# Q and three quarters of V as 26 products of sums of blocks in a one-core attention block

## The chip, the cores and the metric

The kernel runs on one core of a Trainium2 chip. The metric is the device time of one execution in microseconds; the time before is the median of three runs.

## The reference, cut to what matters

Two sequences of 512 tokens, width 512, pass through an attention with 32 heads of 128 and then a small gated feed-forward part, all in float32. The change touches only the projections to Q and V:

```python
x = _layernorm(hidden)                 # (2, 512, 512)
q = rms_norm(x @ Wq + bq, gq)          # (2, 512, 4096), normed over all 4096
k = rms_norm(x @ Wk + bk, gk)
v = x @ Wv + bv
attn = softmax(q_h @ k_h.T * scale)    # for each of 32 heads
out = (attn @ v_h) @ Wo + bo
x = hidden + _layernorm(out)           # then the feed-forward part
```

## The kernel before

The work runs in stages. First the tokens of each sequence are normed and transposed into four tiles of 128 features by 512 tokens (`norm_transposed`, L150). Then `project` (L194) makes Q, and after it K, in eight chunks `g` of four heads. A chunk is the product of both sequences' tokens with 512 weight columns. It is done by seven products of sums of 2x2 blocks instead of eight: `weight_sums` (L183) makes four sums of weight blocks on GpSimd, `token_sums` (L172) makes four sums of token blocks on VectorE once, in the opening of the q stage, and VectorE adds the products up as it reads them from PSUM (L278 to L301). Each of the seven is two heads `j` by two matmuls `c`, so that a chunk is 28 matmuls of 128x128 by 128x512. Every finished head goes to HBM (`keptq`, `keptk`, L237), ScalarE squares it (L235) and GpSimd adds the squares to `accq` or `acck` (L236), from which the norm over 4096 comes. These squares go through `tmp`, four tiles.

Other work is laid beside the q stage: `value_sums` (L322) loads blocks of Wv, makes four sums of them on GpSimd and stores them in `keptw`; `output_sums` (L348) does the like for Wo on VectorE (`keptwo`). Beside the k stage, Q is scaled (`scalings`, L368, two of the steps at each call of `between`) and stored again in `keptqs`.

V is made by `values` (L433), as a list of steps. For each of four parts `p` of 1024 columns, 14 entries of seven kinds of product with two token tiles each give 28 steps, each of two matmuls (L458) with a later exit by VectorE or ScalarE (L466 to L486). Of these 112 steps 28 run ahead of the head loop, 28 in the first eight iterations, and 56 in the 36 iterations after.

The head loop (L696) has 64 iterations, one for a head of one sequence. TensorE makes the scores of the next head (L515), a small matmul for the softmax's sum (L548), V steps and products with Wo (`through_wo`, L615, L621, again seven for eight), and then the weighted values (L571). ScalarE copies the scores (L516) and takes the exponential (L562); VectorE finds the maximum (L525, L526), subtracts it (L559) and sums (L534, L542); GpSimd reduces the maximum over partitions (L528). The products with Wo leave PSUM by ScalarE (L627) and are added in SBUF by DMAs that GpSimd issues (L628).

The order on TensorE, VectorE, ScalarE and GpSimd is the order in which the program issues (`IN_ORDER`, L25). The order on SP, the queue of most DMAs, is the scheduler's. PSUM has eight banks of 128x512 float32, taken by turns.

## Time and profile before

| What | us |
|---|---|
| median of three runs | 1321.91 (1321.35 to 1324.21) |
| the profiled execution | 1322.88 |
| its span, first to last instruction | 1321.1 |
| TensorE busy | 1294.2 (98%) |
| VectorE busy | 973.5 (74%) |
| ScalarE busy | 533.4 (40%) |
| GpSimd busy | 481.7 (36%) |
| first product of the q stage starts | 12.52 |
| first product of the k stage starts | 208.20 |
| first V product starts | 402.19 |

In a line of the profile, PE, DVE, ACT, POOL and SP are TensorE, VectorE, ScalarE, GpSimd and SyncE; PEld is TensorE's weight load. A float32 matmul shows as two records. In a timeline or in the chain, the first number is the start in us from the span's start and the second is the length in us; `x8` counts instructions drawn together; the bracket at the end gives the idle time of that engine just before, and what ended it. L numbers are lines of the kernel before.

### The profile page before, as it was taken

To read this page: it belongs to the slowest core of one execution; us is meant where nothing else is said; L and a number is where in the kernel's file an instruction comes from. 1 tells how busy PE (TensorE), PEld (TensorE's weight loads), DVE (VectorE), ACT (ScalarE), POOL (GpSimd) and SP (SyncE) were. 2 spreads that over 40 slices of the span, in tenths; PEclk is the share of its full clock that TensorE was granted. 3 is DMA by queue.
4 is the path that set the end of the run, shared out by engine and by line. 5 is a ranking of instruction groups with operands and counts; after the bars stand their busy time and mean duration, and the time that the engine had idled before them with its cause. 6 is when DMAs were issued, how large, how long until landed. Compare 5 with 4: busy or idle time off the path is not lost.

```text
span 1321.1 us, 11827 instructions
## 1 busy us (share of the span) xinstructions
PE 1294.2 (98%) x3532; PEld 651.5 (49%) x3532; DVE 973.5 (74%) x1235; ACT 533.4 (40%) x732; POOL 481.7 (36%) x368
## 2 busy tenths in 40 slices
PE   7999999999999999999999999999999999999996
PEld 3444444444444444455555555555555555544453
DVE  7565654888565478888777786886877887899666
ACT  5222222322221234354444545455444566544253
POOL 3799897556762011111123231322322322211002
PEclk9999999999999999999999999999999999999999
DMA  8799978599997765533456566566557565520101
GB/s 288 240 326 310 338 268 273 199 342 309 321 344 265 248 199 181 180 120 98 153 152 183 141 182 160 140 183 168 161 151 197 132 156 139 146 64 24 36 5 64
DMA packets 146127, 250.45 MB, mean 190 GB/s; under 512 B 11792, under 2 KB 39568, under 8 KB 146064
## 3 DMA queue, kind: packets, MB, share of 16 engines
q1 hardware_dynamic: 135408, 230.31, 52.3%
q0 software_dynamic: 10080, 18.35, 8.4%
q10 hardware_dynamic: 576, 1.05, 0.2%
q8 instruction: 28, 0.46, 0.2%
q14 instruction: 35, 0.29, 0.1%
HBM read 147.43 MB, written 83.89 MB: 175 GB/s over the span
## 4 chain that ended last, share of the span: by engine, by line
PE 90%; DVE 7%; ACT 2%; DMA 1%; issue 1%; SPq 0%; ACTq 0%; DVEq 0%
PE pss L515 15%; PE o L571 15%; PE v L458 15%; PE p_q L215 15%; PE p_k L215 15%; PE psw L621 10%; PE psy L665 2%; DVE quarters L534 1%; DVE s L559 1%; PE hg L816 1%; ACT s L562 1%; DVE y L655 1%; PE psd L548 1%; PE f L823 1%; DVE m L525 1%
## 5 line engine op out<-in xcount | busy, mean ns | idle before, releaser
L528 POOL PARTITION_ALL_REDUCE top<-m x64 | 119.0, 1860 | 616.8 <-DVE m L526 616.8
L516 ACT ACTIVATE s<-pss,rk 128x512 f32<-128x512 f32 x256 | 175.9, 687 | 320.2 <-PE pss L515 314.7
L571 PE MATMUL o<-s,v 128*128 128x512 f32 x512 | 231.4, 594 | 5.9 <-ACT s L562 2.6
L515 PE MATMUL pss<-qh,kh 128*128 128x512 f32 x512 | 230.2, 592 | 0.0
L515 PEld LDWEIGHTS pss<-qh,kh 128*128 128x128 f32 x512 | 97.3, 190 | 122.5 <-issue 121.5
L571 PEld LDWEIGHTS o<-s,v 128*128 128x128 f32 x512 | 96.2, 190 | 112.0 <-issue 96.9
L534 DVE TRANSPOSE_TENSOR_REDUCE quarters<-s 128x64 f32<-128x2048 f32 x64 | 147.3, 2301 | 0.0
L559 DVE TENSOR_TENSOR s<-s,top 128x2048 f32<-128x2048 f32 x64 | 146.0, 2281 | 0.0
L562 ACT ACTIVATE s<-s 128x2048 f32<-128x2048 f32 x64 | 121.7, 1902 | 13.7 <-DVE s L559 13.6
L458 PE MATMUL v<-w_v,t 128*128 128x512 f32 x256 | 116.8, 600 | 0.0
L550 DVE RECIPROCAL inv<-psd 128x16 f32<-128x16 f32 x64 | 16.4, 256 | 127.5 <-PE psd L548 127.5
L236 POOL TENSOR_TENSOR accq<-accq,sq_q 128x512 f32<-128x512 f32 x62 | 80.9, 1306 | 36.7 <-ACT sq_q L235 35.2
L236 POOL TENSOR_TENSOR acck<-acck,sq_k 128x512 f32<-128x512 f32 x62 | 85.8, 1388 | 21.5 <-ACT sq_k L235 18.3
L235 ACT ACTIVATE sq_q<-q 128x512 f32<-128x512 f32 x62 | 38.9, 630 | 132.8 <-DVE q L288 69.1
L235 ACT ACTIVATE sq_k<-k 128x512 f32<-128x512 f32 x62 | 38.5, 630 | 133.5 <-DVE k L288 66.0
L458 PE MATMUL v<-w_v,nT_a 128*128 128x512 f32 x192 | 88.3, 601 | 0.0
L621 PE MATMUL psw<-wr,oh 128*128 128x256 f32 x384 | 88.3, 380 | 0.0
L215 PE MATMUL p_k<-t,s_k 128*128 128x512 f32 x192 | 85.0, 592 | 0.0
L215 PE MATMUL p_q<-t,s_q 128*128 128x512 f32 x192 | 85.0, 592 | 0.0
L621 PEld LDWEIGHTS psw<-wr,oh 128*128 128x128 f32 x384 | 72.5, 190 | 19.8 <-issue 11.5
L525 DVE TENSOR_TENSOR m<-s 128x1024 f32<-128x1024 f32 x64 | 77.8, 1215 | 4.7 <-ACT s L516 4.7
L458 PEld LDWEIGHTS v<-w_v,t 128*128 128x128 f32 x256 | 46.7, 190 | 49.3 <-issue 49.0
(182 smaller groups left out, 1781.9 us busy)
## 6 DMA issues: line engine op xcount, KB each, us to landing
keptq<-q SPq DMA_DIRECT2D x64, 256.0 KB, 6.4
q<-keptq SPq DMA_DIRECT2D x16, 1024.0 KB, 6.5
w_v<-keptw SPq DMA_DIRECT2D x32, 512.0 KB, 3.9
keptk<-k SPq DMA_DIRECT2D x64, 256.0 KB, 6.6
keptqs<-q SPq DMA_DIRECT2D x64, 256.0 KB, 6.7
qh<-keptqs SPq DMA_DIRECT2D x64, 256.0 KB, 3.0
kh<-keptk SPq DMA_DIRECT2D x64, 256.0 KB, 2.7
keptv<-o_v SPq DMA_DIRECT2D x64, 256.0 KB, 3.8
```

The source lines that it names most:

```text
L215: nc.tensor.matmul(ps, a[:, c, ts(j, P)], x[c], start=(c == 0), stop=(c == 1))
L236: nc.gpsimd.tensor_tensor(accs[b], accs[b], sq, ALU.add)
L458: nc.tensor.matmul(ps, x[c][:, ts(t, P)], w[:, c, :], start=(c == 0), stop=(c == 1))
L515: nc.tensor.matmul(ps, kk[i][:, ts(k, P)], qs[i], start=True, stop=True)
L516: nc.scalar.activation(s[:, k, :], ps, AF.Copy, scale=rks[b][:, k : k + 1])
L525: nc.vector.tensor_tensor(m, s[:, 0:2, :], s[:, 2:4, :], ALU.max)
L528: nc.gpsimd.partition_all_reduce(ms[i], m[:, 0, :], P, ReduceOp.max)
L534: nc.vector.tensor_reduce(quarters.rearrange("p k j -> p (k j)"), ss[i].rearrange("p k (j r) -> p (k j) r", r=32), AX.X, ALU.add, apply_tr ...
L559: nc.vector.tensor_tensor(s, s, top.unsqueeze(1).to_broadcast([P, NT, 512]), ALU.subtract)
L562: nc.scalar.activation(ss[i], ss[i], AF.Exp)
L571: nc.tensor.matmul(po, vs[b, c][:, k, ts(j, P)], ss[i][:, k, :], start=(k == 0), stop=(k == NT - 1))
L621: nc.tensor.matmul(ps[:, t, :], a, right_of[i, g][:, j, :], start=(j == 0), stop=(j == 1))
```

## The change

Q and the parts 0 to 2 of V are no longer made by 28 matmuls for a 2x4 by 4x4 arrangement of blocks, but by 26. One side of a block of work has 2x4 pieces of 128x512 (in V the weights of a part, in Q the transposed tokens of both sequences), the other 4x4 pieces of 128x128 (in V one sequence's tokens, in Q a chunk's weights). `X_ADDS` lists 18 sums of the wide pieces (numbers 8 to 25), `W_ADDS` 28 sums of the narrow ones (16 to 43); "~" also turns the sign. `STEPS` is the order of one block's work, with times in units of a product: 26 products by number, some added onto another's bank, 9 copies out of PSUM on ScalarE, 11 joins on VectorE, all of which read one operand from PSUM, and 8 last sums that give the results. Four of the last sums have both inputs in SBUF.

There are six V blocks (part by sequence), then eight Q blocks, one for a chunk. `values_and_queries` puts every instruction at a time (26 to a block) and issues them sorted by it. Sums of raw Wv pieces go to VectorE and those with a sum in them to GpSimd, and the same for the weight pieces of Q; in the first block the tokens' 28 sums go to VectorE, and the second sequence's are dealt to both by turns. The second sequence is loaded behind Wv on SP, and normed and transposed inside the first block. The pieces of Wq of a chunk are made one block ahead, the wide token sums of Q in the last V block, and the sums of Wv's last part (`value_sums`) and of Wo (`output_sums`, in eight smaller steps) beside the Q blocks. The pieces live in two pools that are given back before the k stage, and six pools of the later stages take their place.

`project` is left with K alone, and makes `token_sums` at its start. `values` is left with part 3: 28 steps, 14 ahead of the head loop and 14 in its first eight iterations. None run after.

The diff, cut to its core:

```diff
+POOLS = (("vpool", 4), ("hpool", 3), ("xpool", 4), ("spool", 3), ("gpool", 2), ("upool", 7))
...
+X_ADDS = (
+    (8, 5, "-", 6), (9, 1, "-", 8), (10, 2, "+", 3), (11, 3, "-", 7), (12, 2, "+", 11), (13, 11, "-", 0),
...
+W_ADDS = (
+    (16, 8, "+", 10), (17, 4, "+", 16), (18, 1, "+", 13), (19, 11, "-", 15), (20, 10, "+", 11), (21, 20, "-", 15),
...
+STEPS = (
+    (0.00, "product", 17, None, 9, 17), (1.00, "product", 22, None, 7, 14), (1.93, "copy", 17),
+    (2.00, "product", 15, None, 10, 18), (2.66, "copy", 22), (3.00, "product", 24, None, 2, 19), (3.41, "copy", 15),
...
+    (24.00, "product", 25, 19, 21, 43), (24.92, "last", 6, "s6", "+", "s8"), (25.00, "product", 4, 10, 25, 0),
+    (26.17, "last", 7, "s7", "-", "s8"), (27.43, "join", 1, "s15", "-", "p1"), (28.68, "last", 1, "s1", "-", "s19"),
+    (29.93, "join", 25, "p25", "-", "s23"), (31.19, "last", 4, "p4", "+", "s25"),
+    (32.44, "last", 0, "s0", "+", "s25"),
...
-            (nc.sync, nc.scalar)[b].dma_start(out=xts[t], in_=x[b, ts(t, P), :])
+            if b == 0:
+                nc.sync.dma_start(out=xts[t], in_=x[b, ts(t, P), :])
         return xts
...
-        if len(xTs) < B:
-            load_next(1)
-            leave = open_chunk(0, "ps")
-            second = norm_transposed(xs[1], "a1", "aux")
-            leave()
-            xTs.append(second())
-            leave = open_chunk(1, "ps")
-            sums.extend(token_sums(xTs))
-            leave()
+        load_next(1)
+        open_chunk(0)()
+        sums.extend(token_sums(xTs))
+        open_chunk(1)()
...
+        def values_and_queries(small_pieces, pieces):
...
+            def add(engine, to, p, op, q):
+                engine.tensor_tensor(to, p, q, ALU.subtract if op == "-" else ALU.add)
+                if op == "~":
+                    nc.scalar.activation(to, to, AF.Copy, scale=-1.0)
...
+                def step(kind, node, *args):
+                    if kind == "product":
+                        on, one, two = args
+                        if on is None:
+                            banks[node], left[node] = free.pop(0), uses[node]
+                        nc.tensor.matmul(banks[root[node]], seconds[two], firsts[one], start=on is None, stop=closing[node, one], skip_group_check=True)
+                    elif kind == "copy":
+                        nc.scalar.copy(tile_of(node), banks[root[node]])
+                        read(node)
+                    else:
+                        p, op, q = args
+                        how = (value(p), ALU.add if op == "+" else ALU.subtract, value(q))
+                        if kind == "last":
+                            finish[0](node, *how)
+                        else:
+                            to = values[node] if p == f"s{node}" else tile_of(node)
+                            nc.vector.tensor_tensor(to, how[0], how[2], how[1])
+                        for v in (p, q):
+                            if v[0] == "p":
+                                read(int(v[1:]))
...
+            def token_piece(b, to, p, op, q, engine):
+                v = tokens[b]
+                v[to] = small_pieces.tile([P, P], F32, tag="s", name=f"x{to}_{b}")
+                add(engine, v[to], v[p], op, v[q])
...
+            def value_piece(p, to, a, op, c, engine):
+                v = wv_pieces[p]
+                v[to] = pieces.tile([P, 512], F32, tag="f", name=f"wv{p}_{to}")
+                add(engine, v[to], v[a], op, v[c])
...
+            def value_out(p, b):
+                def finish(node, first, op, second):
+                    f, t = divmod(node, NT)
+                    pool, tag = ((qpool, "q"), (kpool, "k"))[node % 2]
+                    o = pool.tile([P, 512], F32, tag=tag, name=f"v{p}_{b}_{node}")
+                    nc.vector.tensor_tensor(o, first, second, op)
+                    nc.sync.dma_start(out=keptv[b, 2 * p + f, t], in_=o)
+
+                return finish, lambda node: None
...
+            rows_pieces = {b * NK + k: xTs[b][k] for b in range(B) for k in range(NK)}
+
+            def rows_piece(to, p, op, q, engine):
+                v = rows_pieces
+                v[to] = pieces.tile([P, 512], F32, tag="f", name=f"xr{to}")
+                add(engine, v[to], v[p], op, v[q])
...
+            def query_piece(g, to, p, op, q, engine):
+                v = wq_pieces[g]
+                v[to] = small_pieces.tile([P, P], F32, tag="s", name=f"wq{g}_{to}")
+                add(engine, v[to], v[p], op, v[q])
...
+                def finish(node, first, op, second):
+                    b, j = divmod(node, GH)
+                    h = g * GH + j
+                    o = outs[node] = qpool.tile([P, 512], F32, tag="q", name=f"q{b}_{h}")
+                    nc.vector.scalar_tensor_tensor(o, first, bq[:, h : h + 1], second, ALU.add, op)
+                    nc.sync.dma_start(out=keptq[b, h], in_=o)
+
+                def squared(node):
+                    b, j = divmod(node, GH)
+                    h, o = g * GH + j, outs[node]
+                    if b not in begun:
+                        begun.add(b)
+                        nc.scalar.activation(accq[b], o, AF.Square)
+                    else:
+                        sq = tt(f"sq_q{b}_{h}")
+                        nc.scalar.activation(sq, o, AF.Square)
+                        nc.gpsimd.tensor_tensor(accq[b], accq[b], sq, ALU.add)
...
+            V, G_ = nc.vector, nc.gpsimd
+            nv = B * LATE
+            load_values(0)
+            for t in range(NT):
+                nc.sync.dma_start(out=xs[1][t], in_=x[1, ts(t, P), :])
+            nc.sync.dma_start(out=vec, in_=vecs)
+            (apply0, turn0, leave0), (apply1, turn1, leave1) = (first_norm(b) for b in range(B))
+            for t in range(NT):
+                apply0()
+                turn0()
+            for t in range(NT):
+                leave0(t)
+            for n, a in enumerate(W_ADDS):
+                at(need["w", a[0]] - 6, lambda a=a: token_piece(0, *a, V))
+            for n, a in enumerate(X_ADDS):
+                at(need["x", a[0]] - 6.1, lambda a=a, e=(V, G_)[n > 3 and n % 2]: value_piece(0, *a, e))
+            for t in range(NT):
+                at(2.2 + 2 * t, apply1)
+                at(6.3 + 2 * t, turn1)
+                at(8.4 + 2 * t, lambda t=t: leave1(t))
+            for n, a in enumerate(W_ADDS):
+                at(15.4 + 0.37 * n, lambda a=a, e=(V, G_)[n % 2]: token_piece(1, *a, e))
+            at(2.5, lambda: nc.sync.dma_start(out=row, in_=rows.partition_broadcast(P)))
+            at(20.3, constants)
+            for p in range(1, LATE):
+                at(26 * (2 * p - 2) + 1.5, lambda p=p: load_values(p))
+                for n, a in enumerate(X_ADDS):
+                    at(26 * (2 * p - 1) + 4.3 + 1.05 * n, lambda p=p, a=a, e=(V, G_)[max(a[1], a[3]) >= 8]: value_piece(p, *a, e))
+            for n, a in enumerate(X_ADDS):
+                at(26 * (nv - 1) + 4.3 + 1.05 * n, lambda a=a, e=(V, G_)[max(a[1], a[3]) >= 8]: rows_piece(*a, e))
+            for g in range(NG):
+                n = nv + g
+                at(26 * (n - (2 if g == 0 else 1)) + 0.5, lambda g=g: load_queries(g))
+                for i, a in enumerate(W_ADDS):
+                    raw = max(a[1], a[3]) < 16
+                    at(26 * (n - 1) + 7.2 + 0.68 * i, lambda g=g, a=a, e=(G_, V)[raw]: query_piece(g, *a, e))
+            for c in range(2):
+                at(26 * (nv + 1 + 2 * c) + 3.5, lambda c=c: value_sums(LATE, c))
...
+            for g in range(WG):
+                at(26 * (nv + g) + 0.3, lambda g=g: load_rows(g, rows_of[g % 2]))
+                for i in range(8):
+                    at(26 * (nv + g + 1) + 1.2 + 3 * i, lambda g=g, i=i: output_sums(g, rows_of[g % 2], i))
+            at(26 * (nv + NG - 1) + 0.6, lambda: wk0.append(load_w(wk[:, ts(0, GH * P)], "w_k0")))
+            for p in range(LATE):
+                for b in range(B):
+                    block(2 * p + b, f"v{p}_{b}", wv_pieces[p], tokens[b], value_out(p, b))
+            for g in range(NG):
+                block(nv + g, f"q{g}", rows_pieces, wq_pieces[g], query_out(g))
+            for _, _, work in sorted(events, key=lambda e: e[:2]):
+                work()
...
+        with ExitStack() as scope:
+            pools = [
+                scope.enter_context(tc.tile_pool(name=name, bufs=bufs, reuse_waits="tile"))
+                for name, bufs in (("spieces", 56), ("fpieces", 32))
+            ]
+            values_and_queries(*pools)
+        vpool, hpool, xpool, spool, gpool, upool = (
+            ctx.enter_context(tc.tile_pool(name=name, bufs=bufs, reuse_waits="tile"))
+            for name, bufs in POOLS
+        )
-        for g in project(xTs, sums4, wq, bq, steps[:, 0, :], "q", [(qpool, "q")], keptq, accq, weight_sums(wq0, "q0")):
-            if g == 0:
-                nc.sync.dma_start(out=row, in_=rows.partition_broadcast(P))
-            if g == 2:
-                nc.vector.tensor_scalar(nbthr, bthr, -1.0, None, ALU.mult)
-                nc.vector.tensor_tensor(gqk, vec[:, 3, :], vec[:, 4, :], ALU.mult)
-            if g == NG - 2:
-                k_parts = weight_sums(load_w(wk[:, ts(0, GH * P)], "w_k0"), "k0")
-            value_sums(g // 2, g % 2)
-            if 0 < g <= WG:
-                output_sums(g - 1)
-            if g < WG:
-                load_halves(g)
-        for g in project(xTs, sums4, wk, bk, steps[:, 1, :], "k", [(kpool, "k"), (upool, "u")], keptk, acck, k_parts, between=scale_some):
-            if g == 0:
...
+        k_parts = weight_sums(wk0[0], "k0")
...
-            todo = [(p, tiles, i, x) for p in range(NG // 2) for tiles in ((0, 1), (2, 3)) for i, x in order]
+            todo = [(p, tiles, i, x) for p in (LATE,) for tiles in ((0, 1), (2, 3)) for i, x in order]
...
-        for n in range(28):
+        for n in range(14):
             next(v_steps)()
-            if n in (2, 4):
-                key_scales(n // 2 - 1)
-            if n == 12:
+            if n in (2, 3):
+                key_scales(n - 2)
+            if n == 4:
                 for i in range(3):
                     fetch(i)
-            if n == 18:
+            if n == 7:
                 scores(0)
                 top_of(0)
         for c in range(2):
             for b in range(B):
                 fetch_v(b, c)
         combining, held = [], []
-        left = 28 * (NG // 2 - 1)
+        left = 14
         po = None
...
-            want = 28 * (i + 1) // G if i < G else 28 + 56 * (i + 1 - G) // (5 * G - 4)
-            while left and 84 - left < want:
+            while left and 14 - left < 14 * (i + 1) // G:
```

## The prediction

> **What bounds the kernel now.** I read the page's busy rows first, then the chain of work that ended last in order of time, then timelines of single engines where the change lands.

> ```profile
> PE 1294.2 (98%) x3532; PEld 651.5 (49%) x3532; DVE 973.5 (74%) x1235; ACT 533.4 (40%) x732; POOL 481.7 (36%) x368
> ...
> PE   7999999999999999999999999999999999999996
> ...
> POOL 3799897556762011111123231322322322211002
> ```

> TensorE is never idle after the first slice of 33 us, so only matmuls taken away, or gaps opened in TensorE, move the time. GpSimd is busy in the first ten slices, where the change puts its sums, and nearly idle after.

> ```profile
> 22.80 185.40 PE p_q L215 x432
> 208.20 24.04 PE p_k L215 x56
> ```

> Two lines of the chain in order of time: 432 matmul records in 185.4 us, 0.4286 us each; a float32 128x512 matmul is two records, 0.857 us. The q stage has 448 records (192.0 us) and ends at 208.2, so 16.2 us of it are not products.

> ```profile
> 64.71 0.80 DVE L352 TENSOR_TENSOR wo<-wo 128x512 f32<-128x512 f32 x1
> 65.54 1.64 DVE L353 TENSOR_TENSOR wo<-wo,wo 128x512 f32<-128x512 f32 x1
> 67.21 1.64 DVE L354 TENSOR_TENSOR wo<-wo,wo 128x512 f32<-128x512 f32 x1
> 68.89 1.64 DVE L355 TENSOR_TENSOR wo<-wo 128x512 f32<-128x512 f32 x1
> ...
> 72.62 0.69 DVE L278 TENSOR_TENSOR u_q<-p_q,u_q 128x512 f32<-128x512 f32 x1 [0.90 <-PE p_q L215]
> ...
> 68.27 1.71 POOL L329 TENSOR_TENSOR a_v<-a_v,a_v 128x512 f32<-128x512 f32 x1
> 70.06 1.60 POOL L330 TENSOR_TENSOR s_v<-a_v,a_v 128x512 f32<-128x512 f32 x1
> 71.62 1.27 POOL L331 TENSOR_TENSOR a_v<-a_v,a_v 128x512 f32<-128x512 f32 x1
> ```

> Timelines of VectorE and GpSimd. A VectorE sum with both inputs in SBUF takes 1.64 us instead of 0.69 while GpSimd works, and GpSimd's takes 1.71 instead of 1.27. They take turns, one pair every 1.67 us. L278, which reads PSUM, is not slowed with GpSimd busy.

> ```profile
> 1124.44 3.60 PE L571 MATMUL o<-s,v 128*128 128x512 f32 x8
> ...
> 1134.98 3.60 PE L571 MATMUL o<-s,v 128*128 128x512 f32 x8
> ...
> 1144.59 0.70 PE L571 MATMUL o<-s,v 128*128 128x512 f32 x1 [0.63 <-ACT s L562]
> ```

> TensorE late in the head loop, where no V product is left. A head with two output products (L621) takes 10.54 us (1134.98 less 1124.44), its matmuls' own time; a head with one takes 9.61 and waits for the exponential (L562).

> **The change part by part.** *Products.* A block is 26 matmuls of 128 instead of 28. Eight Q chunks and six V blocks (three parts, two sequences) lose 28 matmuls: **-24.0 us**. The instruction order of the changed kernel shows 364 such matmuls, so this part is certain.

> *Opening.* Before, the first product starts at 12.5 and the 16.2 us include it. After, x0's four loads stand alone at the head of SP's queue (Wv's eight, then x1's four behind them; x1 came by ScalarE's queue), which gains perhaps 1 us; but two wide and two narrow VectorE sums now stand between the transposed tokens and the first product (0.60, 0.69, twice 0.29: 1.9 us). I take 12 to 13. Then VectorE's queue is long. Up to the result that frees the bank for product 8, the fifth product from the block's end, it holds 35 sums of 128x128 (L862 is the row, 0.285 us, four in 0.90, so 0.205 each: 7.2), 11 of 128x512 at 0.60 (6.6), 9 reads of PSUM at 0.60 (5.4), x1's four norms at 1.06 (4.2) and two copies (1.2): 24.6 us. GpSimd makes seven wide pieces meanwhile, and each can hold a VectorE sum up to 1.04 us (1.64 less 0.60): 6 more. From about 10 us that is 40.6; five products and a wait follow, so block 0 ends near 46, against 22.3 us of products. What is queued behind: ScalarE's norms of x1 wait for VectorE, the bank copies stand behind them in order, and TensorE waits for the banks. 23.7 us outside products instead of 16.2: **+7.5**.

> *The shared turns.* GpSimd's 128x128 sum is not in the trace. Bounds: a quarter of the row's 1.27 us is 0.32. [...] I take 0.41 as the pitch. A steady Q block then holds on GpSimd 18 narrow sums (7.4) and 8 square sums (L236, 1.23 apart: 9.8), and on VectorE, with both inputs in SBUF, 4 results (0.55 each), 10 raw weight sums (0.15) and 8 output-weight sums (0.28): 5.9. Together 23.1 us against TensorE's 22.3. In blocks q1 and q3 the value sums add 4 x 1.23 to make 28.0. Over q1 to q6 that is 2 x 5.7 + 4 x 0.8 = 14.6; q0 and q7 have slack, I take **+12**. In the V stage an odd block has 12 wide sums on GpSimd (14.8) and 10 on VectorE (5.5), 20.3: hidden. The last V block also makes the first weight pieces: 22.1 + 7.0 = 29.1, partly wanted late in q0: **+3**.

> [...] Row: a pair costs 1.67 us. [...]

> *VectorE alone* in a Q block: 19 results and joins (8 at 0.66, 11 at 0.60: 11.9) and 18 sums (about 4.6): 16.5 of 22.3, hidden as long as its turns come. ScalarE: 9 copies (0.58) and 8 squares (0.63), 10.3, hidden by the same block.

> *DMA.* 48 stores of V and Wv's loads leave the head loop for the V stage: 3 MB a block, 135 GB/s, hidden. Q: 5 MB a block, 7 in q1 and q3 (314 GB/s; the page's best slice shows 344). SP loads the value pieces in q0 and has them before GpSimd asks. Scaled-Q loads and late V weights that were spread over the q stage now fall into the first k chunk, with the wait for SP that this makes; the first thing wanted behind them, the third k weights, has two chunks (48 us) of cover. Cost nil, 0 to 3 if the cover fails.

> *Start of K.* The token sums (L177 to L180), eight VectorE sums from SBUF, were made in the opening and are now made when K starts, after chunk 0's first results (7.2 us in), while GpSimd makes eight weight sums. At 1.67 us the sixth, which product 6 needs, is done at 17.2; TensorE is there at 14.6: **+2.6** (0 to 6).

> *Head loop.* 1.5 V products a head go from heads 8 to 43. Nine of these heads are left with one output product and take 9.61 us for 8.83 of matmuls: +7.0. Before, six heads (15, 16, 23, 24, 39, 40) lost 3.9 us to late banks, as the 1.49 us wait shows below; VectorE no longer reads V there, so that goes, and the exponential is late next. Heads 0 and 4 keep one V product: +1.5. Net **+4.7**.

> ```profile
> 776.14 1.10 PE L571 MATMUL o<-s,v 128*128 128x512 f32 x2 [1.49 <-ACT w L627]
> ```

> The 14 V steps left ahead of the loop (24 us) still cover the first head's chain (ScalarE 0.69, VectorE 1.9, GpSimd 1.86, VectorE 2.28: under 7 us).

> **Sum:** -24.0 + 7.5 + 12 + 3 + 2.6 + 4.7 = **+5.8**. The profiled execution took 1322.88 us for a span of 1321.1; it lies 1.0 above the median of 1321.91. I put the change on the median: 1327.7, say **1328**.

> **The rivals.**
> 1. *The turns fit (faster).* If the narrow GpSimd sum takes 0.32 or less, a Q block's shared work is 21.5, under 22.3, and the stalls of q0 to q7 shrink to the two value blocks; if VectorE also slips its short sums in between GpSimd's, those go too. Then -24.0 + 4.5 (opening with half the waits) + 4.7, and 0 to 4 for the rest: -15 to -11, about **1309**. The point is 22.3 us of shared work a block. For: POOL has slack in the v stage, and the operations are short. Against: the 1.64 us rows.
> [...]
> 3. *The head loop turns VectorE-bound* without the V products. VectorE needs 8.4 us a head (rows L534, L559, L525, L526, L552, L577, L542, L550) of 9.6. The heads from 43 on show that it does not; no more than +3.
> 4. *It doesn't do what it says:* excluded by the instruction order.

> **How the numbers follow.** The forecast, 1319 to 1338, 0.52; rival 1, 0.27; rival 2 and what lies between, 0.19; rival 3, 0.02. What a measurement here can tell from no change is about 0.2%, 2.6 us: 1319.3 to 1324.5. Of the forecast 0.11 lies inside that, of rival 1 0.01; so faster 0.26, same 0.12, slower 0.62. The range leaves out a tenth on each side: 1306 (below rival 1's middle) to 1350 (short of rival 2).

> **What would show it.** Right: 3476 TensorE records; block 0 ending near 46 us; about 22.5 us a block in V; 25 to 28 us in q1 and q3 with TensorE waiting on a VectorE result; VectorE SBUF sums of 1 to 1.6 us beside GpSimd; two or three us lost 15 us into K; heads at 9.6 and 10.5 from head 8. Wrong: Q blocks all at 22.3 (rival 1), or all above 26 (rival 2), or heads longer than 10.6.

## The result, and the profile after

The changed kernel takes 1354.53 us (median of four, 1350.87 to 1356.81) against 1322.12 of the kernel before beside it: 1.024 times as long, 95% interval 1.0214 to 1.0266. The prediction said 1328, and 1350 at most. The profiled execution took 1354.19 us for a span of 1352.3, 31.2 longer than the 1321.1 of before.

The page after: busy rows, then TensorE's, GpSimd's and the clock's rows of the 40 slices.

```profile
PE 1290.3 (95%) x3476; PEld 641.9 (47%) x3476; DVE 1102.7 (82%) x1479; ACT 584.3 (43%) x840; POOL 553.1 (41%) x513
...
PE   5899999899999999999999999999999999999996
...
POOL 1524578988675655711111223332333223211002
PEclk8899999999999999999999999999999999999999
```

The 3476 records are there, 56 fewer than before. But TensorE is busy for only 3.9 us less (1294.2 less 1290.3) where 24.0 were taken away, and idle for 35.1 us more (1352.3 less 1290.3, against 1321.1 less 1294.2). Part of that is records that got longer, which the clock's row shows; the prediction had no term for it. By stage, from the starts of the blocks on TensorE's timeline (before, K starts at 208.04 and V at 402.02; the 208.20 and 402.19 given above are the ends of the records just before them, so what lay outside products was 16.0 us and not 16.2):

| Stage | before | after | change | predicted |
|---|---|---|---|---|
| products, 14 blocks | | 56 records fewer | -24.0 | -24.0 |
| opening: what lies outside products to the end of block 0 | 16.0 | 31.0 (13.0, then 40.3 less 22.3) | +15.0 | +7.5 |
| V blocks 1 to 5 | 111.4 of products | 117.2 (22.9, 22.3, 22.9, 22.3, 26.8) | +5.8 | +3 |
| Q blocks | 178.3 of products | 192.5 (22.3, 26.2, 23.8, 27.4, 23.4, 23.8, and 45.7 for the last two) | +14.2 | +12 |
| K | 194.0 | 202.7 | +8.7 | +2.6 |
| V steps ahead, head loop, rest | 775.1 | 786.5 | +11.5 | +4.7 |
| sum | | | +31.2 | +5.8 |

*Opening.* TensorE's timeline after; then VectorE's and ScalarE's ahead of the first gap, and two of VectorE's rows further on.

```profile
16.93 1.12 PE L484 MATMUL bank<-wv,x 128*128 128x512 f32 x2 [0.23 <-DVE x L459]
24.45 3.75 PE L484 MATMUL bank<-wv,x 128*128 128x512 f32 x4 [6.39 <-issue]
...
44.94 1.16 PE L484 MATMUL bank<-wv,x 128*128 128x512 f32 x2 [2.62 <-DVE v L564]
46.93 5.49 PE L484 MATMUL bank<-wv,x 128*128 128x512 f32 x6 [0.84 <-DVE c_v L495]
```

```profile
18.12 1.38 DVE L459 TENSOR_TENSOR x<-x,x 128x128 f32<-128x128 f32 x1
19.42 1.75 DVE L459 TENSOR_TENSOR wv<-wv,wv 128x512 f32<-128x512 f32 x1
21.09 0.68 DVE L177 BATCH_NORM_STATS2 st_a<-x 128x6 f32<-128x512 f32 x1
...
29.02 0.69 DVE L526 COPY nT_a<-bank 128x512 f32<-128x512 f32 x1 [1.75 <-PE bank L520]
...
44.12 0.67 DVE L564 TENSOR_TENSOR v<-c_v,bank 128x512 f32<-128x512 f32 x1
```

```profile
18.24 0.31 ACT L461 ACTIVATE x<-x 128x128 f32<-128x128 f32 x1 [6.40 <-DVE x L459]
18.46 0.57 ACT L486 COPY c_v<-bank 128x512 f32<-128x512 f32 x1
22.08 0.29 ACT L180 ACTIVATE rs_a<-mv_a,epst 128x1 f32<-128x1 f32 x1 [3.06 <-DVE mv_a L178]
```

Read VectorE's rows first, then ScalarE's, then TensorE's. A narrow sum takes 1.38 us and a wide one 1.75 beside two wide sums of GpSimd (2.54 us from 18.09 on; just before, VectorE's narrow sum took 0.28 and its wide one 0.68); x1's norm stands behind them on VectorE; ScalarE waits 3.06 for it; the bank copies (L486) stand behind that in ScalarE's order; and TensorE has no free bank for 6.39 us. VectorE in turn waits 1.75 us at 29.02 for x1's transposed tokens, which TensorE made late.

Behind the gaps TensorE is slow: four records take 3.75 us instead of 1.88, and later six take 5.49 instead of 2.74. This is the granted clock (PEclk, last but two of the columns: share of a stretch at full speed) in the same profile:

```profile
20.00:30.00 10.00, 5.55 (x11) 2.80 (x12) 7.63 (x26) 6.77 (x14) 0.62 (x1) 0.66 0.12 46
30.00:40.00 10.00, 10.00 (x33) 4.97 (x32) 9.39 (x21) 1.66 (x3) 5.05 (x5) 1.00 0.09 34
40.00:53.70 13.70, 10.24 (x17) 3.96 (x16) 13.34 (x32) 0.78 (x2) 7.46 (x13) 0.75 0.24 89
53.70:144.00 90.30, 89.69 (x209) 39.35 (x208) 62.52 (x87) 21.10 (x36) 32.25 (x24) 1.00 0.35 122
```

*Q.* TensorE's timeline in q1 and, in its last row, q2; VectorE's and GpSimd's in q1:

```profile
208.63 1.13 PE L484 MATMUL bank<-xr,wq 128*128 128x512 f32 x2 [1.89 <-DVE q L597]
209.59 1.82 PE L484 MATMUL bank<-xr,w_q 128*128 128x512 f32 x2
211.21 1.91 PE L484 MATMUL bank<-xr,wq 128*128 128x512 f32 x2
...
238.43 1.10 PE L484 MATMUL bank<-xr,wq 128*128 128x512 f32 x2 [1.23 <-POOL wq L459]
```

```profile
199.55 1.48 DVE L383 TENSOR_TENSOR wo<-wo,wo 128x256 f32<-128x256 f32 x1
200.96 0.67 DVE L495 TENSOR_TENSOR c_q<-c_q,bank 128x512 f32<-128x512 f32 x1
201.55 3.30 DVE L459 TENSOR_TENSOR wq<-w_q 128x128 f32<-128x128 f32 x3
```

```profile
199.43 1.32 POOL L362 TENSOR_TENSOR a_v<-a_v,a_v 128x512 f32<-128x512 f32 x1
200.71 1.45 POOL L363 TENSOR_TENSOR a_v<-a_v,s_v 128x512 f32<-128x512 f32 x1
202.12 3.86 POOL L609 TENSOR_TENSOR accq<-accq,sq_q 128x512 f32<-128x512 f32 x3
```

Three narrow VectorE sums last 3.30 us beside three wide sums of GpSimd (3.86 us), where one at 208.83, with GpSimd idle, takes 0.28; the join that reads a bank (L495), beside GpSimd's L363, keeps its 0.67. That is what the prediction described, sizes included. In q1 and q3 TensorE waits for a result of VectorE; in q2 and q4 to q6 it waits 0.82 to 1.23 us for a narrow sum of GpSimd itself, as in the row at 238.43.

*K and heads.* Two waits in K, each with slow records behind it, and the first head; TensorE, after.

```profile
380.17 7.97 PE L249 MATMUL p_k<-t,s_k 128*128 128x512 f32 x14 [2.38 <-DVE t L212]
...
539.96 8.80 PE L249 MATMUL p_k<-nT_a,w_k 128*128 128x512 f32 x16 [2.46 <-DVE q L409]
...
602.62 3.70 PE L861 MATMUL o<-s,v 128*128 128x512 f32 x8 [2.28 <-ACT s L852]
```

Fourteen records at full speed are 6.17 us. The first wait was predicted (2.6, fifteen us into K). The second is VectorE waiting for a late load of Q to be scaled, which had been costed at nil; SP's waits from 200 to 570 us show what its issue stood behind, stores of scaled Q that had not landed (us in total, times, longest; the changed kernel, then the kernel before from 200 to 410 us):

```profile
SPq L404 <- DMA keptqs<-q: 43.4, 16, 5.1
```

```profile
SPq L375 <- DMA keptqs<-q: 46.0, 17, 4.7
```

The third wait of TensorE is the exponential of head 0.

### The profile page after: what moved, and what is told of

Its sections match the earlier page's. It is cut to its first block, busy times and chain, and to the rows that moved or that the text cites. A ratio compares the mean times of both kernels' runs of the same rounds, so it can differ in the third digit from the quotient of the medians.

```text
span 1352.3 us, 12232 instructions
## 1 busy us (share of the span) xinstructions
PE 1290.3 (95%) x3476; PEld 641.9 (47%) x3476; DVE 1102.7 (82%) x1479; ACT 584.3 (43%) x840; POOL 553.1 (41%) x513
## 4 chain that ended last, share of the span: by engine, by line
PE 47%; DVE 9%; ACT 4%; issue 1%; ACTq 0%; DVEq 0%
PE o L861 15%; PE pss L805 14%; PE psw L911 8%; PE v L736 3%; ACT s L852 3%; PE psy L955 2%; PE p_k L249 2%; DVE quarters L824 1%; DVE s L849 1%; PE hg L1104 1%; DVE m L815 1%; DVE y L945 1%; PE f L1111 1%; DVE r L842 0%; DVE acc_y L945 0%
## 5 line engine op out<-in xcount | busy, mean ns | idle before, releaser
L861 PE MATMUL o<-s,v 128*128 128x512 f32 x512 | 233.1, 598 | 11.9 <-ACT s L852 11.7
L484 PE MATMUL bank<-wv,x 128*128 128x512 f32 x264 | 126.1, 621 | 14.8 <-issue 6.4
L484 PE MATMUL bank<-xr,wq 128*128 128x512 f32 x256 | 124.5, 601 | 9.1 <-DVE q L597 5.0
L852 ACT ACTIVATE s<-s 128x2048 f32<-128x2048 f32 x64 | 121.8, 1904 | 24.3 <-DVE s L849 24.2
L270 POOL TENSOR_TENSOR acck<-acck,sq_k 128x512 f32<-128x512 f32 x62 | 85.3, 1380 | 29.8 <-ACT sq_k L269 26.9
L609 POOL TENSOR_TENSOR accq<-accq,sq_q 128x512 f32<-128x512 f32 x62 | 85.7, 1398 | 16.6 <-ACT sq_q L608 16.0
L484 PEld LDWEIGHTS bank<-wv,x 128*128 128x128 f32 x264 | 51.2, 198 | 82.0 <-issue 66.2
L484 PEld LDWEIGHTS bank<-xr,wq 128*128 128x128 f32 x256 | 48.7, 192 | 73.4 <-issue 53.7
L486 ACT COPY c_v<-bank 128x512 f32<-128x512 f32 x54 | 31.4, 585 | 89.5 <-PE bank L484 89.5
```

The costliest lines, as they stand in the source:

```text
L484: nc.tensor.matmul(banks[root[node]], seconds[two], firsts[one], start=on is None, stop=closing[node, one], skip_group_check=True)
L609: nc.gpsimd.tensor_tensor(accq[b], accq[b], sq, ALU.add)
L852: nc.scalar.activation(ss[i], ss[i], AF.Exp)
L861: nc.tensor.matmul(po, vs[b, c][:, k, ts(j, P)], ss[i][:, k, :], start=(k == 0), stop=(k == NT - 1))
```

## The experiments

Runs 1 to 9 are single executions. They are read by their stages; their totals come from three chips and are not set against each other. A stage varies by itself: where the code of the opening is that of the changed kernel, block 0 took 37.7 to 40.8 us, and the last V block 25.1 to 26.9. Theory A: each stage pays for its own stalls, of the named queue, and the half clock comes on top.

**1. Q without GpSimd's sums of squares.**

```diff
                         nc.scalar.activation(sq, o, AF.Square)
-                        nc.gpsimd.tensor_tensor(accq[b], accq[b], sq, ALU.add)
```

> The changed kernel without GpSimd's sums of the squares of Q (the line accq + sq; the squares themselves are still made, their sum is left out). Theory A (VectorE's SBUF sums and GpSimd's take turns, and in q1 to q5 both together want more than TensorE's 22.3 us): 62 sums of 1.23 to 1.5 us leave GpSimd, 8 or so a block, so the shared work falls from 23 to some 13 us a block, in q1 and q3 from 28 to 18; every Q block at 22.3, q1 and q3 too (26.2 and 27.4 now), the Q stage about 13 us shorter (191.7 to 178 or 179) and its granted clock 1.00 throughout; the whole about 1341. Theory B (the blocks wait for PSUM banks, ScalarE's copies or the transfers of the value sums, GpSimd only stands beside): q1 and q3 stay above 25, the whole within 3 us of 1354. [...]

Measured: Q blocks of 22.3, 23.3, 22.3, 23.7, 22.3, 22.3 and together 44.6 for the last two; the stage 181.0 instead of 192.5, granted clock 1.00 (0.98 in the changed kernel). Groups of VectorE in q1 to q7, the changed kernel first (after the bar: busy us, mean ns of one; then idle time before):

```profile
L459 DVE TENSOR_TENSOR wq<-w_q 128x128 f32<-128x128 f32 x60 | 26.4, 456 | 13.8 <-DMA w_q<-in_wq 13.8
L383 DVE TENSOR_TENSOR wo<-wo,wo 128x256 f32<-128x256 f32 x24 | 19.4, 807 | 0.0
L597 DVE SCALAR_TENSOR_TENSOR q<-c_q,vec,bank 128x512 f32<-128x512 f32 x21 | 15.6, 743 | 1.5 <-PE bank L484 0.3
```

```profile
L597 DVE SCALAR_TENSOR_TENSOR q<-c_q,vec,bank 128x512 f32<-128x512 f32 x21 | 15.6, 745 | 1.9 <-PE bank L484 1.3
L459 DVE TENSOR_TENSOR wq<-w_q 128x128 f32<-128x128 f32 x60 | 17.5, 308 | 16.4 <-DMA w_q<-in_wq 16.4
...
L383 DVE TENSOR_TENSOR wo<-wo,wo 128x256 f32<-128x256 f32 x24 | 10.6, 441 | 0.0
```

With GpSimd's wide sums gone, the same VectorE sums fall from 456 to 308 ns and from 807 to 441; results that read a bank stay at 743 and 745. Of the stage's 14.2 us, 11.5 hang on GpSimd's sums of squares, 3.4 of them as half clock that did not come. So it is theory A, and banks and copies (B) are out as the main cause. But the run takes away two things at once, the turns and the time that these sums hold GpSimd's own queue, in which the narrow sums that TensorE waits for stand; it does not part them. Of the rest, q1 has a wait of 0.71 us for GpSimd and q3 two for ScalarE's copies (0.24 and 0.70).

**2. Filling the wait in K with matmuls.**

```diff
         open_chunk(1)()
+        warm = pt("warm")
+        for n, cols in enumerate((512, 512, 256)):
+            nc.tensor.matmul(warm[:, 0:cols], xTs[0][n][:, 0:P], xTs[1][n][:, 0:cols], start=True, stop=True)
```

> The changed kernel with three extra matmuls (512, 512 and 256 columns, 2.14 us of records, results read by nobody) on TensorE just where it waits 2.38 us for the token sum t2 at the start of K. Theory A (the wait costs twice: its own length, and then 14 records at half clock because TensorE stood idle): the extra work costs nothing, the wait falls to 0.3 us or less, the next 14 records take 6.1 us and not 7.97, and the K stage ends 1.8 us sooner (202.9 to 201.1). Theory B (the slow records have another cause, a late bank or the clock being cut for the load's sake): the records behind still take 8 us, K is as long as it was or 2 us longer.

Measured: the wait 0.23, the fourteen records 6.28 instead of 7.97, as theory A has it; the K stage 201.6, with a wait of 3.33 for the late load further on. But the run doesn't show what it was made for: runs 6, 8 and 9 have the whole wait of 2.36 to 2.38 and also 6.28. The slow records come in some executions and not in others, with the same wait. That is taken up under the hardware below.

**3. The opening without the token sums of sequence 0.**

```diff
                 v = tokens[b]
+                if b == 0:
+                    v[to] = v[p]
+                    return
```

> The changed kernel without the 28 token sums of sequence 0 (VectorE, 128x128, and the sign change on ScalarE; raw pieces take their place in the products, so block 0's and later sequence-0 V results are of other data). Theory A (block 0 of 40.7 us is VectorE's queue in order: sums, x1's norms behind them, ScalarE behind those, the banks behind ScalarE): 7.2 us leave VectorE's queue and with them one stall's half clock, block 0 takes 30 to 34. Theory B (the eight Wv transfers, or GpSimd's seven wide sums one behind the other, set it): 39 to 41. Theory C (TensorE's own order, its banks, sets it): 40 to 41. The other blocks unchanged to 0.5 us.

Measured: block 0 takes 29.2 instead of 40.3, a little more gain than theory A had; the other V blocks 22.9, 22.3, 22.9, 22.3, 25.1. 7.2 us less in VectorE's queue gave 11.1, and block 0 has no half clock. Transfers (B) and TensorE's own order (C) fall.

**4. The V steps and the sums of head pairs dealt otherwise.**

```diff
-        for n in range(14):
+        for n in range(10):
             next(v_steps)()
...
-            if n == 4:
+            if n == 3:
...
-            if n == 7:
+            if n == 6:
                 scores(0)
...
+        v_at = {0: 3, 11: 1, **{i: 2 for i in range(1, G)}}
...
-            while left and 14 - left < 14 * (i + 1) // G:
+            for _ in range(v_at.get(i, 0)):
...
-            if n4 == 0 and 0 < c <= 2 * WG:
-                head_sums(c - 1)
+            if n4 == 1 and 0 < c <= 2 * WG:
+                half_sums = head_sums(c - 1)
+            if n4 in (1, 3) and 0 < c <= 2 * WG:
+                next(half_sums)
```

> The changed kernel with its 28 steps of the last part of V dealt otherwise: 10 ahead of the head loop and not 14, 3 in head 0 as the kernel before had there, 2 in each of heads 1 to 7, 1 in head 11; scores of head 0 one step sooner; and the four sums of head pairs cut in two halves, in the second and the fourth of the four heads and not all in the first. The work is the same. Theory A (the head loop lost 11.5 us because V's products that covered the exponential are gone: 2.28 in head 0, 3.1 in heads 4, 8 and 12 behind the sums of head pairs, 0.75 in each head with a single output product): the 2.28 us wait goes, heads 4, 8 and 12 lose under 0.3 each, one head of 9.61 less; V and heads 5 to 7 us shorter than 786.4, the whole about 1348. Theory B (the loop is VectorE's and each head is as long as VectorE's work in it): 784 to 787, the loss only moves to other heads. Theory C (fewer steps ahead uncover the first head's chain of scores, maximum, exponential): a new wait of 3 to 6 us before head 0, and nothing gained.

Measured: V and heads 779.0 instead of 786.5, 7.5 less. Head 0 waits no more; heads 4, 8 and 12 take 10.53, 10.65 and 10.54 instead of 12.04, 11.70 and 11.11 (head 7 now 11.28). Eleven heads with one output product stay at 9.60. Theory A; the run does not part its three edits. In the same run the late load in K cost a wait of 5.83.

**5. K: token sums first, the load of Q issued later.**

```diff
-        open_chunk(0)()
+        leave = open_chunk(0)
         sums.extend(token_sums(xTs))
+        leave()
...
-                if j == GH - 1 and n + 3 < NG * B:
-                    four_of(n + 3)
+                if j == 1 and 0 < n < NG * B - 2:
+                    four_of(n + 2)
```

> The changed kernel with two edits of order in the K stage, no work changed: the eight token sums stand on VectorE ahead of the results of the first K chunk and not behind them, so they can run while TensorE makes that chunk; and the load of the next four Q heads to be scaled is issued two scalings later, when the stores that it must wait for have landed, so that SP does not stand behind them. Theory A (the two waits of TensorE in K, 2.38 us for t2 and 2.46 to 5.8 us behind a late scaled-Q load, with some 1.8 us of half clock after each, are the 8.9 us that K lost): both waits under 0.3 us, the K stage 194 to 196 us and not 202.9, granted clock 1.00 in it. Theory B (GpSimd, busy with eight weight sums at that point, holds VectorE's token sums up wherever they stand): the wait at t2 moves to the results of the first chunk and to the banks, K 200 or more. Theory C (the transfers themselves are late, not their issue): the second wait stays, K about 199.

Measured: K 197.0 instead of 202.7, clock 1.00. The waits did not go to 0.3 but to 1.20 and 1.21, the first moved to the chunk's results as B has it (L284 in the line, TensorE), and no half clock came behind them:

```profile
377.87 3.67 PE L249 MATMUL p_k<-t,s_k 128*128 128x512 f32 x8 [1.20 <-DVE k L284]
```

The late load is judged over all runs. With the old issue, TensorE waited in late K in seven executions out of nine: 2.46 in the changed kernel, 5.09, 3.33, 1.55 and 5.83 in runs 1 to 4, 3.73 in run 7, 5.07 (there for K's weights) in run 9; only 0.29 in run 6 and nothing in run 8, where K took 197.2 and 196.9. With the later issue (runs 5, 10, 11) it was 1.21, 0.22 and nothing. So the issue that stands behind a store not yet landed is the likely cause, as far as three executions against nine can show, and how late it is varies. In the kernel before, SP waited as long for the same stores (46.0 us) and TensorE did not wait; what took that cover away was not tried.

**6. The value sums in q0 and q7.**

```diff
-                at(26 * (nv + 1 + 2 * c) + 3.5, lambda c=c: value_sums(LATE, c))
+                at(26 * (nv + (0, 7)[c]) + 3.5, lambda c=c: value_sums(LATE, c))
```

> The changed kernel with the two groups of four value sums (GpSimd, 128x512, with their loads and stores) in q0 and q7 and not in q1 and q3. Theory A (shared turns of VectorE and GpSimd): q1 and q3 fall from 26.2 and 27.4 to the 23.8 of q2 and q4, so 6 us less there; q0 and q7, which have no output-weight sums, keep under 24, so the Q stage is 4 to 6 us shorter. Theory B (the loads and stores of the value sums on SP and the DMA queues set q1 and q3): the same gain there, but q0 and q7 grow by as much, because the transfers go with the sums. Theory C (a stall there has nothing to do with them): q1 and q3 stay at 26 and 27.

Measured: Q blocks 22.3, 25.3, 23.5, 23.5, 23.4, 23.5, 23.4, 22.3, the stage 187.3, 5.2 less, of which 3.4 is half clock that did not come. q3 falls by 3.9 as A has it, q0 and q7 don't grow, so it isn't the transfers. q1 keeps 25.3: it waits 1.22 us for a result and 1.29 for a weight sum of GpSimd. That the sums pushed into q0 delay these is likely, but not shown.

**7. The squares added by transfers.**

```diff
-                        nc.gpsimd.tensor_tensor(accq[b], accq[b], sq, ALU.add)
+                        nc.gpsimd.dma_start(out=accq[b], in_=sq, accum_op=ALU.add)
```

> The changed kernel with the 62 sums of squares of Q made by accumulating transfers (issued on GpSimd, as the head loop adds its output products) and not by GpSimd's own sums; the result is the same. Theory A (what costs is the turn at SBUF that VectorE and GpSimd share, and a transfer takes none): as without the sums, Q blocks 22.3 to 23.7, the stage 180 to 182. Theory B (GpSimd's queue is what is full: an accumulating transfer has to wait for the one before it on the same sum, 4.3 us each in the head loop, and the narrow sums stand behind the issue in order): Q blocks 24 to 30, no better than 191.7. Theory C (banks or copies): 191 to 192.

Measured: a span of 1403.7, the Q stage 243.5, q1 to q4 at 27.7, 39.1, 30.2 and 35.6 us. GpSimd's waits between 190 and 330 us (us in total, times, longest):

```profile
POOL accq L609 <- DMA accq<-sq_q: 33.5, 8, 8.8
```

Theory B: each transfer waits for the one before it on the same sum, and the weight sums stand behind it on GpSimd. VectorE's output-weight sums that took 807 ns take 509 here, so they were held up less, and the stage still grew by 51 us: GpSimd's queue in its order was a cost by itself.

**8. The opening dealt otherwise.**

```diff
-                at(need["w", a[0]] - 6, lambda a=a: token_piece(0, *a, V))
+                at(need["w", a[0]] - 6, lambda a=a, e=(V, G_)[n in token0_g]: token_piece(0, *a, e))
...
-                at(2.2 + 2 * t, apply1)
+                at(8.0 + 2.5 * t, apply1)
```

> The changed kernel with the opening dealt otherwise, the same sums made: x1's norms, turns and copies 6 us later in the order, 14 of sequence 0's 28 token sums on GpSimd and not on VectorE, 8 of the 18 value pieces on GpSimd (7 before, later ones now), sequence 1's token sums from 22 on. Theory A (block 0 is VectorE's queue in order, with ScalarE and the banks behind x1's norms, and two stalls' half clock): VectorE's queue loses some 3 us of sums and the norms go behind what block 0 needs, so no stall of 2 us is left; block 0 takes 27 to 33 instead of 40.7, and block 1 stays under 24. Theory B (the sums on VectorE and GpSimd only take turns, so that dealing them out wins nothing): 37 to 41. Theory C (x1's work, put later, is what block 1 then waits for): block 0 shorter by 5 or more, block 1 longer by as much.

Measured: first product at 11.5, block 0 in 26.8 instead of 40.3, block 1 in 22.8. TensorE, and the windows to the first product and over block 0; last, block 0 of the changed kernel:

```profile
15.01 7.89 PE L484 MATMUL bank<-wv,x 128*128 128x512 f32 x18
```

```profile
0.00:11.50 11.50, 4.10 (x16) 2.99 (x16) 8.21 (x31) 6.71 (x12) 2.02 (x9) 1.00 0.83 280
11.50:38.30 26.80, 26.49 (x68) 11.79 (x69) 26.09 (x62) 10.78 (x21) 18.61 (x24) 1.00 0.45 167
```

```profile
13.00:53.30 40.30, 30.21 (x68) 13.27 (x69) 36.86 (x88) 10.00 (x21) 16.82 (x21) 0.83 0.30 113
```

Eighteen records without a gap where there were 6.39 us of one. Theory A. VectorE (the third of the busy times) is still full, 26.09 of 26.80 us, but with less to do: 62 instructions where there were 88 in 36.86. The run changes the share of VectorE and the order of x1's norms together, so how the 13.5 us divide is not shown; run 3, which changes the share alone, gave 11.1. The Q stage of this run took 196.1 (q2 26.5), 3.6 more than in the changed kernel; why was not looked into.

**9. The Q blocks' sums dealt out again.**

```diff
-                at(26 * (nv - 1) + 4.3 + 1.05 * n, lambda a=a, e=(V, G_)[max(a[1], a[3]) >= 8]: rows_piece(*a, e))
+                at(26 * (nv - 1) + 4.3 + 1.05 * n, lambda a=a, e=(G_, V)[n in (3, 13)]: rows_piece(*a, e))
...
-                    raw = max(a[1], a[3]) < 16
-                    at(26 * (n - 1) + 7.2 + 0.68 * i, lambda g=g, a=a, e=(G_, V)[raw]: query_piece(g, *a, e))
+                    on_v = i in (0, 2, 3, 4, 13, 14, 19, 23, 25)
+                    at(26 * (n - 1) + 7.2 + 0.55 * i, lambda g=g, a=a, e=(G_, V)[on_v]: query_piece(g, *a, e))
```

> The changed kernel with the weight sums of each Q block dealt out again (19 on GpSimd and not 18, another nine on VectorE and not ten, the later ones started sooner: 0.55 and not 0.68 of a matmul apart), the eight output-weight sums 2.8 and not 3 apart, and of the 18 sums of x's rows in the last V block 16 on GpSimd and not 12. The same sums are made. Theory A (in q2, q4 and q5 the 1.3 us a block over 22.3 are single sums that come late because of the order on the two engines, not of their sum of work, and so is the last V block's 2.9 to 4.9): last V block 22.3 to 23.5 (25.1 to 27.2 now), q2, q4 and q5 near 22.8 (23.5 to 24.2 now), q1 and q3 above 24 as before, the Q stage 186 to 189. Theory B (the shared work itself fills the block): every block within 0.3 us of what it was. Theory C (GpSimd becomes the bound with 16 row sums of 1.27 us): the last V block grows to 28 or more.

Measured: last V block 22.3 (26.8), q2 to q6 at 23.9, 26.6, 23.0, 23.2, 23.0, but q1 27.8: the stage 192.2 (192.5), no shorter. The last V block is theory A; q1 is 1.6 us longer and has a half-clock stretch, so the Q stage alone is a miss.

**10 and 11. The edits of 8, 4, 5 and 6 together; then with 9.**

> The edits of the runs on the opening, the heads, the K start and the value sums together. Theory A (each stage pays for its own stalls, and they add up): from 1354.5, the opening gives 15, the heads 7.5, K 5.7, the value sums 4.4, some 2 in the last V block: 1320, which is the kernel before within 0.3%. Theory B (what is gained ahead of a stage is given back behind it, because its transfers or buffers are then late): 1330 or more.

> The run above with the Q blocks' sums dealt out again too. Theory A: the last V block and six Q blocks give another 5 to 8: 1312 to 1315, some 0.6% faster than the kernel before, so that of the 24.0 us of products a third is kept, the rest being the opening's 5, Q's 5, K's 3 and the head loop's 4. Theory B: as the run above, 1320.

Measured: run 10 takes 0.9988 of the time before (0.9971 to 1.0005), no difference; run 11 takes 0.9906 (0.9882 to 0.9931), 1313.1 us against 1323.5 beside it, and is the fastest. Its busy row and clock row:

```profile
PE 1275.7 (97%) x3476; PEld 639.1 (49%) x3476; DVE 1112.8 (85%) x1453; ACT 585.3 (45%) x840; POOL 576.5 (44%) x539
...
PEclk9999999999999999999999999999999999999999
```

Its account against before: products -24.0, opening +0.8, V +1.3, Q +6.8 (q1 25.3, q2 to q6 23.0), K +1.6, heads +4.0: -9.5, as the spans differ (1311.6 and 1321.1). In run 11 what one stage gains is not given back in the next.

## Why the prediction was wrong

The sign and the list of places were right; the sum was 25.4 us short: 7.3 in the opening, 7.0 in the head loop, 6.1 in K, 2.8 in V and 2.2 in Q. The steps that failed are the sum of VectorE's queue in the opening, the covers that were taken to hold in K and in head 0, and half clock behind a stall, which had no term at all.

- **Products, -24.0:** right.
- **Opening, +7.5:** the largest miss, 15.0. The step that failed took VectorE as never idle, and the five products behind it as running at full speed but for one wait. The result that frees the bank for product 8 was put at 40.6 us. It is L564 at 44.12, and product 8 starts at 44.94: 4.2 us late. VectorE's 46 sums up to there took 20.0 us instead of 13.8, so the 6 us allowed for turns were right; but VectorE stood idle for some 3.6 us from 10 to 44.8, 1.75 of it at 29.02. The engines wait for each other in a circle there (norms, transposes, copies, banks), which the sum of one queue does not show. From 44.94 to the block's end the five products took 8.4 us instead of the 5.4 counted with a wait. Half clock is 4.6 us of block 0's products, where the kernel before had 1.5 at its start.
- **Head loop, +4.7:** single-product heads and late banks as predicted. Missing were head 0's exponential, which three V steps had covered (2.28; "still cover the first head's chain" was the false step), and heads 4, 8 and 12, where the sums of head pairs put VectorE behind (3.1). Run 4 gave back 7.5. About 1.4 of the 11.5 stay open.
- **K, +2.6:** the wait for the token sums was 2.38, as predicted; with only that, runs 6 and 8 show K 2.9 to 3.2 longer. The failed step is the cost put at "nil, 0 to 3 if the cover fails": the cover named was that of K's weights, and what came late was the scaled-Q loads. It brought 2.46 of wait, and 3.5 of half clock came after the two.
- **V, +3:** 5.8: 1.2 in blocks 1 and 3, and in the last 2.7 of waits and 1.8 of half clock.
- **Q, +12:** right in cause, with the reservation of run 1, and near in size (14.2), in part by luck. Less 3.4 of half clock, the waits were 10.8. In q1 and q3 they were 2.1 and 3.4 where 5.7 each was counted; in q2 and q4 to q6 1.1 to 1.5 where 0.8 was. No run shows the 0.41 us put as the pitch of GpSimd's narrow sums; after the change one alone takes 0.45 and two in a row 0.87, and the 144 on weights of Q average 0.53. Rival 2's mark, all Q blocks above 26, was passed by q1 and q3 alone, at 26.2 and 27.4; the others took 22.3 to 23.8.

Half clock alone is 13.3 us of the changed kernel's records and 1.5 of the kernel before: 11.8 of the 25.4 us. The range ended at 1350 with no room for it. Two slips in the prediction's sums change nothing: 185.4 / 432 is 0.4292, and 7.0 - 3.9 + 1.5 is 4.6.

## What to carry to other kernels

A saving on the bounding engine is real only as far as the engines that feed it keep up: of the 24.0 us of products here, run 11 kept 9.5 and the changed kernel none. Add up what each queue holds, what stands behind its slowest instruction, and where the engines wait for each other in a circle. Here 1.88 us or more of idle time on TensorE within one slot of 3.41 us (next section) were followed by half clock in 53 of 56 cases, which costs a busy TensorE another 1.7 us, so stalls were better short and apart. When work is taken from a place where it covered a chain, find the chain and lay some of the remaining pieces there first, as run 4 did with three V steps in head 0.

## What the hardware showed unexpectedly

In these traces the slow records come by all or nothing. The same six records of the last V block, after the same wait of 1.51, TensorE in the changed kernel and in run 6:

```profile
165.32 4.51 PE L484 MATMUL bank<-wv,x 128*128 128x512 f32 x6 [1.51 <-DVE c_v L495]
```

```profile
162.93 2.84 PE L484 MATMUL bank<-wv,x 128*128 128x512 f32 x6 [1.51 <-DVE c_v L495]
...
370.93 6.28 PE L249 MATMUL p_k<-t,s_k 128*128 128x512 f32 x14 [2.38 <-DVE t L212]
```

1.7 to 1.8 us more, or 0.1: three of ten executions paid at that wait of 1.51, three of six at 2.36 to 2.38 in K, two of nine at the exponential's 2.28.

```profile
376.93:380.34 3.41, 1.03 (x4) 0.20 (x3) 3.38 (x3) 0.00 (x0) 3.33 (x3) 1.00 0.52 201
380.35:383.76 3.41, 3.41 (x5) 1.33 (x6) 3.41 (x3) 0.00 (x0) 3.41 (x3) 0.50 0.03 5
```

```profile
369.13:372.55 3.42, 1.62 (x4) 0.87 (x5) 3.39 (x4) 0.00 (x0) 3.42 (x3) 1.00 0.13 49
372.55:375.96 3.41, 3.41 (x9) 1.52 (x8) 3.41 (x5) 1.04 (x2) 3.08 (x3) 1.00 0.10 37
```

In the changed kernel the whole wait lies in one slot, and the next is at half clock; in run 6 part of it fell in the slot before, and nothing follows. In the changed kernel alone, up to 1240 us and behind slots at full clock, the six slots with 2.27 to 3.41 us of idle TensorE and the one with 1.89 were followed by half clock, the one with 1.88 (head 0) and the one with 1.22 were not. Over all thirteen traces, from 13 to 1240 us and behind slots at full clock: of the slots with 2.0 us or more of idle TensorE all 46 were followed by half clock, of those with 1.88 to 1.92 seven of ten, of those with 1.0 to 1.87 none of 48. Short waits in one slot add up: the last V block's 1.51 follows one of 0.78. A slot at half clock cost a busy TensorE 1.7 us (the fourteen records in 7.97 us and in 6.28). Runs 10 and 11, without such waits, have no such stretch up to 1240 us.
